# Causal side work moved between slots, buffers of the maxima and of the turned outputs exchanged, and a different plan for the first feed-forward

## The chip, the cores and the metric

The kernel runs on one core of a Trainium2 chip. The metric is device time in microseconds (us). A core has TensorE (PE, with its weight loads PEld), VectorE (DVE), ScalarE (ACT), GpSimd (POOL) and SyncE (SP), which here only issues DMAs. Each engine works through its own instructions in the order in which the program gives them.

## What is computed

Two blocks follow each other, each behind a layernorm and with a residual. All data are 32-bit floats. The first takes x of 4 × 1024 × 256:

```python
q, k, v = proj(wq, bq), proj(wk, bk), proj(wv, bv)      # 16 heads of 16
scores = einsum('bhqd,bhkd->bhqk', q, k) / sqrt(16)
attn = softmax(scores + causal_mask)
x = x + einsum('bhqk,bhkd->bhqd', attn, v) @ wo + bo    # on layernorm(x)
```

The second is a stack of two layers on the result's layernorm: attention of 8 heads of 64 in windows of 128 rows that look at their own and the previous window, with normalized and rotated q and k, and then a gated feed-forward (256 to 2 × 682, a × gelu(g), back to 256) behind a layernorm:

```python
h = shift_token(x); q, k, v = split(h @ wqkv)
x = x + local_attention(rotary_xpos(l2norm(q) * qs, l2norm(k) * ksc), v) @ wo
h = layernorm(shift_token(x)) * lg + lb; a, g = split(h @ w1 + b1)
x = x + (a * gelu(g)) @ w2 + b2
```

## The kernel before, in words

**Causal part.** The work is cut into chunks n = −1 to 15. Chunk n is batch b = n // 4 and head group c = n % 4 (4 heads of 16 rows, each in a strip of 32 partitions). Every chunk has 12 slots u. In a slot, `pair` (called twice, for two heads each) issues two kinds of score matmuls at L418: t, the transposed scores of chunk n, and s, the plain scores of chunk n + 1. Chunk −1, the prologue, has only s. From t, ScalarE makes exponentials (L442), and in the diagonal slots GpSimd zeroes what the mask forbids (affine_select, L448); `products` (L481) multiplies them with v two slots later. From s, VectorE takes row maxima, which are put into q as one more row of the contraction, so that the exponentials come out shifted. Slots 0 to 3 and 8 to 11 hold the diagonal piece: there the maximum is a tensor_tensor_reduce with the mask (L430), which also writes a full result that nobody reads, `junk`. In slots 4 to 7 it is a plain tensor_reduce (L436). The scores s and the helper matmuls share four PSUM banks (`pas`), so a matmul into a bank waits until VectorE has read what was there.

**Side work.** Everything else of the causal part is placed by hand: `put(n, u, function)` hangs a call behind slot u of chunk n, and a slot number of 12 or more runs into the next chunk. The functions are:

- `norm` (L258ff): mean and variance of tiles of the next batch on VectorE; `prep_x` (L275): the normalized tiles, on GpSimd for b > 0; `turn_x` (L298): 32 × 32 transposes on VectorE, and in its second call 16 DMAs that finish the transpose into xnT.
- `project`: projections of q and k, 16 matmuls at L252; `spread` (L377): DMAs of q and k rows into the strips; `prep_b`: v; `put_maxima` (L459): the maxima, by a transpose and DMAs.
- `put_out` (L494ff): the output turned by VectorE (L498), reciprocal of the sums (L500), multiplication on GpSimd (L501); `put_oT` (L506): turned back by VectorE into t3 (L510), and four DMAs into oT (L513).
- `out_b` (L517): the product with wo (pr, L252), then the residual: a copy by ScalarE (L533) and an addition by GpSimd (L534), or, for the last four tiles of the last batch, one addition by VectorE (L530). `out_s`: the statistics of the second layernorm (L541, L542); `out_c` (L557): its result into y_sb, on GpSimd.
- `clear_more` (L233 to L235): three memsets on GpSimd for the q and k buffers of later chunks.

The part runs in a manual schedule: each engine keeps the order in which the program calls. After the last slot, leftover side work, the last output and the last out_b, out_s, out_c follow (L694 to L705). Tile pools a1, a2, a4, a5 give 1, 2, 4, 5 buffers to a tag in turn.

**Window part.** One iteration n projects window n, and works on earlier windows: `stage` turns the rotated q and k of one window and the exponentials of another on VectorE (L864, L878), and then issues 16 DMAs into a ring (L895); `weigh` (plo, L1023) waits for them. The feed-forward of a group of four windows is cut into pieces, f_norm, f_hn, f_turn, six f_up (L1155) and four f_down (L1179, with the residual at L1184). `feed(n, place)`, called three times an iteration (place 0 to 2), issues the pieces whose number in F_PLAN is 3n + place − f_start(G); for the first group f_start is 17. If place 0 holds an f_down, it is fed ahead of stage, and otherwise behind it.

Of the kernel before, what the change touches and what calls it, by code (L numbers as in the profile page):

```python
# [10 lines left out]
F32 = mybir.dt.float32  # L11
# [39 lines left out]
def kernel_body(  # L51
# [122 lines left out]
    with actx:  # L174
# [159 lines left out]
        def bias():  # L334

            pb = one("pbias")
            for c in range(2):
                nc.tensor.transpose(
                    pb[:, c * P : (c + 1) * P], rows_c[:, 0, c * P : (c + 1) * P], ident
                )  # L340
            bv = a2.tile([P, 512], F32, tag="junk", name="bv")
            nc.scalar.copy(bv[:, 0:D], pb[:, 0:D])
            po = one("pbias_o")
            for c in range(2):
                nc.tensor.matmul(
                    po[:, 0:D], lhsT=bv[:, c * P : (c + 1) * P], rhs=wo_sb[:, c, :],
                    start=(c == 0), stop=(c == 1),
                )
            nc.vector.tensor_tensor(rows_c[:, 1, :], po[:, 0:D], rows_c[:, 1, :], ALU.add)
# [32 lines left out]
        def pair(n, u, pr):  # L382

            first, final = n < 0, n + 1 == NCH
            if (first or final) and pr:
                return
            th = () if first else range(4) if final else (2 * pr, 2 * pr + 1)  # L390
            sh = () if final else range(4) if first else (2 - 2 * pr, 3 - 2 * pr)

            def bank(pool, h):
                p, tag = ((pat, "t"), (pas, "s"))[pool]
                return p.tile([P, 512], F32, tag=tag, name=f"{'ts'[pool]}_{n}_{u}_{h}")

            todo = []
            if th:
                qb, kt = UNITS_T[u]
                c0 = max(0, kt * P - qb * 512)  # L400
                ts = {h: bank(final and h % 2, h) for h in th}
                for j, h in enumerate(th):
                    r = slice(32 * h, 32 * h + 32)
                    todo.append((j, 0, ts[h][:, c0:512], kTs(n)[r, kt * P : (kt + 1) * P],
                                 qTs(n)[r, qb * 512 + c0 : (qb + 1) * 512]))
            if sh:
                i, piece = UNITS_M[u]
                k0 = piece * 512
                k1 = min(k0 + 512, (i + 1) * P)
                w = k1 - k0  # L410
                diag = k1 == (i + 1) * P and piece == i // 4
                ss = {h: bank(not (first and h % 2), h) for h in sh}
                for j, h in enumerate(sh):
                    r = slice(32 * h, 32 * h + HD)
                    todo.append((j, 1, ss[h][:, 0:w], qTs(n + 1)[r, i * P : (i + 1) * P],
                                 kTs(n + 1)[r, k0:k1]))
            for j, _, o, lhsT, rhs in sorted(todo, key=lambda x: x[:2]):
                nc.tensor.matmul(o, lhsT=lhsT, rhs=rhs, start=True, stop=True)  # L418
            if sh:
                if i >= 4 and piece == 0 and pr == 0:  # L420
                    mxs[n + 1, i] = a5.tile([P, 4], F32, tag="mx", name=f"mx_{n + 1}_{i}")
                for h in sh:
                    first_of_two = i >= 4 and piece == 0
                    if first_of_two:
                        acc = mxs[n + 1, i][:, h : h + 1]
                    else:
                        acc = nmax[:, piece, 4 * h + i % 4 : 4 * h + i % 4 + 1]
                    if diag:
                        junk = a2.tile([P, 512], F32, tag="junk", name=f"junk_{n}_{u}_{h}")
                        nc.vector.tensor_tensor_reduce(  # L430
                            out=junk[:, 0:w], in0=ss[h][:, 0:w], in1=mask_c[:, 512 - w : 512],
                            scale=1.0, scalar=mxs[n + 1, i][:, h : h + 1] if piece else -3.0e38,
                            op0=ALU.add, op1=ALU.max, accum_out=acc,
                        )
                    else:
                        nc.vector.tensor_reduce(acc, ss[h][:, 0:w], AX.X, ALU.max)  # L436
                if piece and (pr or first):
                    del mxs[n + 1, i]
            for h in th:
                if h % 2 == 0:  # L440
                    et = a8.tile([P, 2, 512], F32, tag="et", name=f"et_{n}_{u}_{h}")
                nc.scalar.activation(et[:, h % 2, c0:512], ts[h][:, c0:512], AF.Exp, scale=ASCALE)  # L442
                if h % 2 == 0:
                    continue
                if kt >= 4 * qb:

                    d = et[:, :, c0 : c0 + P]
                    nc.gpsimd.affine_select(  # L448
                        out=d, in_=d, compare_op=ALU.is_ge, fill=0.0, base=0,
                        pattern=[[0, 2], [1, P]], channel_multiplier=-1,  # L450
                    )
                if h == 1:
                    avs_[n, u] = ([], c0)
                avs_[n, u][0].append(et)
# [51 lines left out]
        def put_oT(n, qb):  # L506

            b, c = divmod(n, NC4)
            t3 = a1.tile([P, 512], F32, tag="t3", name=f"t3_{n}_{qb}")
            nc.vector.transpose(t3, avs_.pop((n, "t1", qb)).rearrange("p q s -> p (q s)"))  # L510
            for j in range(4):
                r = (c % 2) * 64 + j * HD
                nc.sync.dma_start(  # L513
                    oT[r : r + HD, c // 2, qb * 512 : (qb + 1) * 512],
                    t3[STRIP * j : STRIP * j + HD, :],
                )

        def out_b(b, t2):
# [7 lines left out]
                        wo_sb[:, c, :], c,  # L526
                    )
            xt = xs[b][:, t0 : t0 + 2, :]
            if b == B - 1 and t2 >= 2:
                nc.vector.tensor_tensor(xt, pr.rearrange("p (i d) -> p i d", i=2), xt, ALU.add)  # L530
                return
            add = a1.tile([P, 2, D], F32, tag="add", name=f"add_{b}_{t2}")
# [33 lines left out]
        def put(n, u, fn, *a):  # L566

            plan[n + u // NU][u % NU].append((fn, a))

        def outs(n, u, b, t2):  # L570
            put(n, u, out_b, b, t2)
            put(n, u + 1, out_s, b, t2)
            put(n, u + 3, out_c, b, t2)

        def quarters(n, b, d, first, *slots):
            for i, u in enumerate(slots):
# [2 lines left out]
        for n in range(NCH):  # L579
            b, c = divmod(n, NC4)  # L580
            more = b + 1 < B
            if n >= 1:
                put(n, 2, put_out, n - 1, 1)
                put(n, 3, put_oT, n - 1, 1)
            if n + 1 < NCH:
                put(n, 4, put_maxima, n + 1, 0)
                put(n, 11, put_maxima, n + 1, 1)
            put(n, 6, put_out, n, 0)
            put(n, 7, put_oT, n, 0)
            if c == 0:  # L590
                if b:
                    quarters(n, b, 1, 3, 0, 2, 4, 6, 8)
                    outs(n, 7, b - 1, 2)
                    outs(n, NU, b - 1, 3)
                    put(n, 1, spread, n + 2, 0)
                    put(n, 3, spread, n + 3, 0)
# [4 lines left out]
                put(n, 9, spread, n + 2, 1)  # L601
                put(n, NU, spread, n + 3, 1)
            if c == 0 and more:
                for i, u in enumerate((5, 7, 9, 10)):
                    put(n, u, norm, b + 1, 2 * i, 2 * i + 2)
                put(n, 8, prep_x, b + 1, 0)
                put(n, 10, turn_x, b + 1, 0, 0)
                put(n, 10, prep_x, b + 1, 1)
                n += 1
                put(n, 0, turn_x, b + 1, 0, 1)  # L610
                put(n, 1, prep_x, b + 1, 2)
                put(n, 2, prep_x, b + 1, 3)
                put(n, 3, turn_x, b + 1, 1, 0)
                put(n, 4, turn_x, b + 1, 1, 1)
                quarters(n, b + 1, 0, 0, 5, 6, 8, 10)
                n += 1
                quarters(n, b + 1, 0, 4, 0, 2, 3, 4)
# [6 lines left out]
                quarters(n, b + 1, 1, 0, 3, 5, 7)  # L624
                n -= 3
            if c == 3:
                outs(n, 9, b, 0)
                outs(n, 11, b, 1)
        n = -1
        plan[n][0] = [(project, (0, 0, i, 3)) for i in range(2)]  # L630
        plan[n][0] += [(spread, (0, 1, nc.scalar)), (spread, (1, 0)), (spread, (1, 1))]
        put(n, 0, clear_more)
        put(n, 4, bias)
        put(n, 3, load_x, 1, 0, NW)
        put(n, 4, put_maxima, 0, 0)
# [15 lines left out]
        with tc.manual_schedule(  # L651
# [42 lines left out]
            for w in range(LAG, 0, -1):  # L694
                products(NCH - 1, NU - w)
            left = [x for u in plan[NCH] for x in u]
            for fn, a in left[0:1]:
                fn(*a)
            put_out(NCH - 1, 1)
            for fn, a in left[1:]:  # L700
                fn(*a)
            put_oT(NCH - 1, 1)
            for fn in (out_b, out_s, out_c):
                for t2 in (2, 3):
                    fn(B - 1, t2)  # L705
# [492 lines left out]
    }  # L1198
    F_END = max(F_PLAN)

    def f_start(G):

        sooner = 6 if G == 0 else 3 if G == len(groups) - 1 else 0
        return 3 * (GRP * G + GRP + 3) + 2 - sooner

    def feed(n, place, ask=False):

        if ask:
            return any(
                fn is f_down  # L1210
                for G in range(len(groups)) for fn, *_ in F_PLAN.get(3 * n + place - f_start(G), [])
            )
        for G in range(len(groups)):
            i = 3 * n + place - f_start(G)
            for fn, *a in F_PLAN.get(i, []):
                fn(G, *a)
            if G == len(groups) // DEPTH - 1:
                if i == 14:
# [139 lines left out]
```

## Time and profile before

| What | us |
|---|---|
| median of 3 runs | 1952.75 (1952.36 to 1958.35) |
| the profiled execution's own time | 1953.46 |
| its span, first to last instruction | 1951.7 |
| mean granted TensorE clock | 0.969 |
| PE / DVE / ACT / POOL busy | 1889.0 / 1347.7 / 1006.9 / 1029.7 |

The span starts at 0; the causal part runs to about 740 us, the window part from there. In the rows of the profile, the number with an x is a count of instructions. A timeline row gives the start, the duration, the engine, the line and what it writes and reads; in square brackets stands how long its engine had been idle before it, and what ended that. The clock of a stretch is the mean of the clock granted to TensorE: 1.00 is full speed, and where it is lower, some of the stretch ran at half speed.

### The profile page before, as it was taken

How to read it: one execution, taken by the hardware profiler on the slowest of the kernel's cores; microseconds unless marked ns; L12 is line 12 of the kernel's file. 1: busy time of each engine (PE TensorE's matmuls, PEld its weight loads, DVE VectorE, ACT ScalarE, POOL GpSimd, SP SyncE). 2: the span in 40 equal slices, each digit the busy share in tenths (PEclk: the TensorE clock that was granted, in tenths of full speed). 3: DMA queues.
4: the chain of work that ended last, by engine and by line, in shares of the span. 5: the costliest groups of instructions: out<-in, count | busy, mean ns of one | idle time of the engine just before them, and what ended most of it. 6: DMA issues, size and time to landing. Idle time of an engine off the chain costs nothing.

```text
span 1951.7 us, 51316 instructions
## 1 busy us (share of the span) xinstructions
PE 1889.0 (97%) x19258; PEld 1031.6 (53%) x19258; DVE 1347.7 (69%) x4092; ACT 1006.9 (52%) x2649; POOL 1029.7 (53%) x1268
## 2 busy tenths in 40 slices
PE   8999999999999978989899999999999999999899
PEld 4333333333333324656566666666666566566575
DVE  6866777677667835666776777776687687678633
ACT  1546555655656653554545555555545554555521
POOL 3222352245224247675765775675676676676621
PEclk8979999998999998999999999999999999999999
DMA  4022011202201011045555565556565555665520
GB/s 120 22 34 76 24 34 33 62 21 38 63 10 29 11 35 67 7 73 92 93 98 90 92 112 96 117 105 114 90 146 111 102 112 104 111 113 104 99 49 22
DMA packets 785127, 142.86 MB, mean 73 GB/s; under 512 B 753536, under 2 KB 775792, under 8 KB 784368
## 3 DMA queue, kind: packets, MB, share of 16 engines
q1 hardware_dynamic: 784624, 139.32, 36.8%
q8 instruction: 153, 2.51, 0.5%
q14 instruction: 94, 0.77, 0.1%
q10 hardware_dynamic: 256, 0.26, 0.1%
HBM read 21.25 MB, written 8.65 MB: 15 GB/s over the span
## 4 chain that ended last, share of the span: by engine, by line
PE 87%; DVE 4%; SPq 3%; POOL 2%; issue 2%; DMA 1%; ACT 1%; DVEq 0%; POOLq 0%; ACTq 0%
PE t L418 15%; PE pag L1155 15%; PE pf L1179 8%; PE av L481 7%; PE pw L1065 6%; PE pq L796 5%; PE pk L796 5%; PE pv L796 5%; PE plo L1023 4%; PE ls L943 4%; PE pp L252 3%; SPq L895 2%; PE pv L252 2%; PE s L418 2%; PE pr L252 2%
## 5 line engine op out<-in xcount | busy, mean ns | idle before, releaser
L442 ACT ACTIVATE et<-t 128x512 f32<-128x512 f32 (+2 forms) x744 | 327.8, 490 | 232.5 <-PE s L418 210.5
L418 PE MATMUL t<-qbuf,kbuf 32*128 32x512 f32 (+2 forms) x1488 | 396.7, 552 | 2.5 <-ACT et L442 2.4
L418 PE MATMUL s<-kbuf,qbuf 16*128 16x512 f32 (+3 forms) x1440 | 382.3, 554 | 1.3 <-DVE mx L436 0.9
L1155 PE MATMUL pag<-hnT,w 128*128 128x512 f32 x704 | 311.9, 592 | 0.8 <-DVE hnT L1139 0.8
L976 ACT ACTIVATE e<-e,lnmx 128x192 f32<-128x192 f32 (+2 forms) x512 | 224.1, 439 | 39.5 <-DVE lnmx L969 39.0
L418 PEld LDWEIGHTS t<-qbuf,kbuf 32*128 32x128 f32 x1488 | 144.1, 189 | 168.9 <-ACT et L442 111.5
L448 POOL TENSOR_SCALAR_AFFINE_SELECT et<-et 128x256 f32<-128x256 f32 x256 | 102.7, 408 | 225.0 <-ACT et L442 224.6
L990 POOL TENSOR_SCALAR e<-e,lrsum 128x192 f32<-128x192 f32 (+2 forms) x512 | 205.8, 425 | 19.9 <-DVE lrsum L987 14.3
L1155 PEld LDWEIGHTS pag<-hnT,w 128*128 128x128 f32 x704 | 131.5, 190 | 142.7 <-issue 135.1
L481 PE MATMUL av<-et,v_sb 128*32 128x256 f32 (+5 forms) x2240 | 186.9, 406 | 6.5 <-POOL et L448 4.7
L436 DVE TENSOR_REDUCE mx<-s 128x1 f32<-128x512 f32 x240 | 153.3, 682 | 56.5 <-PE s L418 54.3
L835 POOL TENSOR_TENSOR rn<-ss,mhalf 128x16 f32<-128x16 f32 x64 | 188.1, 2939 | 5.3
L1179 PE MATMUL pf<-w,act 128*128 128x256 f32 x768 | 173.1, 379 | 0.0
L832 POOL TENSOR_TENSOR rot<-rot,m 128x1024 f32<-128x1024 f32 x64 | 151.2, 2363 | 35.8 <-DVE m L813 30.1
L1179 PEld LDWEIGHTS pf<-w,act 128*128 128x128 f32 x768 | 145.8, 190 | 26.6 <-issue 7.2
L1169 DVE SCALAR_TENSOR_TENSOR act<-pag,cols_sb,ge 128x512 f32<-128x512 f32 x80 | 59.4, 743 | 141.8 <-ACT ge L1168 103.1
L430 DVE CUSTOM_DVE_ANT_0 junk<-s,mask_c 128x512 f32<-128x512 f32 (+3 forms) x240 | 106.8, 485 | 62.7 <-PE s L418 59.4
L418 PEld LDWEIGHTS s<-kbuf,qbuf 16*128 16x128 f32 x1440 | 142.0, 189 | 10.5 <-DVE mx L436 4.4
L430 DVE CUSTOM_DVE_ANT_0 junk<-s,mask_c,mx 128x512 f32<-128x512 f32 (+3 forms) x240 | 120.9, 546 | 37.6 <-PE s L418 36.4
L969 DVE CUSTOM_DVE_ANT_0 e<-ls,mask_h 128x192 f32<-128x192 f32 x408 | 116.8, 351 | 22.5 <-PE ls L943 22.5
L481 PEld LDWEIGHTS av<-et,v_sb 128*32 128x32 f32 x2240 | 45.4, 109 | 164.0 <-issue 113.4
L1065 PE MATMUL pw<-wlo,loT 128*128 128x256 f32 x512 | 127.7, 393 | 1.1 <-ACT loT L1056 0.7
(294 smaller groups left out, 3379.7 us busy)
## 6 DMA issues: line engine op xcount, KB each, us to landing
ring_sb<-turned SPq DMA_DIRECT2D x880, 96.0 KB
qbuf<-dense SPq DMA_DIRECT2D x128, 32.0 KB
oT<-t SPq DMA_DIRECT2D x128, 32.0 KB
x_keep<-x SPq DMA_DIRECT2D x4, 1024.0 KB
xr<-x_keep SPq DMA_DIRECT2D x8, 512.0 KB
out_dram<-y_sb SPq DMA_DIRECT2D x16, 256.0 KB
kbuf<-dense SPq DMA_DIRECT2D x120, 32.0 KB
x<-in_x_dram SPq DMA_DIRECT2D x3, 1024.0 KB
```

Of the source, the lines that this page charges most:

```text
L418: nc.tensor.matmul(o, lhsT=lhsT, rhs=rhs, start=True, stop=True)
L430: nc.vector.tensor_tensor_reduce(out=junk[:, 0:w], in0=ss[h][:, 0:w], in1=mask_c[:, 512 - w : 512], scale=1.0, scalar=mxs[n + 1, i][:, h : ...
L436: nc.vector.tensor_reduce(acc, ss[h][:, 0:w], AX.X, ALU.max)
L442: nc.scalar.activation(et[:, h % 2, c0:512], ts[h][:, c0:512], AF.Exp, scale=ASCALE)
L481: nc.tensor.matmul(av[32 * j : 32 * j + 32, lo:hi], lhsT=v_sb[b % 2][:, kt, VW * (4 * c + j) : VW * (4 * c + j) + STRIP], rhs=ets[j // 2][ ...
L796: nc.tensor.matmul(pq[i], lhsT=lhs[c], rhs=wt[:, c, i * INNER : (i + 1) * INNER], start=(c == 0), stop=(c == 1),)
L835: nc.gpsimd.tensor_tensor(rn[:, :, 0], ss, mhalf, ALU.pow)
L976: nc.scalar.activation(e[:, i, lo:nk], e[:, i, lo:nk], AF.Exp, bias=nmx[:, h : h + 1], scale=-1.0, accum_out=sums[:, h : h + 1],)
L990: nc.gpsimd.tensor_scalar(e[:, i, lo:nk], e[:, i, lo:nk], rsum[:, h : h + 1], 1.0, ALU.mult, ALU.mult)
L1065: nc.tensor.matmul(pw[:, 0:D], lhsT=oT[:, c, :], rhs=wt[:, c, :], start=(c == 0), stop=(c == 3))
L1155: nc.tensor.matmul(pg[half], lhsT=wt[:, c, ff * P : (ff + 1) * P], rhs=hnT[:, c, :], start=(c == 0), stop=(c == 1),)
L1179: nc.tensor.matmul(pf[:, 0:D], lhsT=act[:, f, i * P : (i + 1) * P], rhs=wt[:, f, :], start=(f == 0), stop=(f == NF - 1),)
```

## The change

1. `junk` has one buffer instead of two; t3, the output turned back, has two instead of one. The small tile bv takes the buffer of `add`.
2. Side work is placed in other slots: put_oT from slots 3 and 7 to 4 and 8; for c = 0, norm from 5, 7, 9, 10 to 3, 5, 7, 9, prep_x from 8, 10 and slots 1, 2 of the next chunk to 7, 9 and 0, 2 of it, turn_x from 10 and (next chunk) 0, 3, 4 to 10, 11 and (next chunk) 3, 5; out_s and out_c of out_b(b − 1, 2), which stays in slot 7, from 8 and 10 to 12 and 14; for c = 3, the first out_b from slot 9 to 10 with its out_s and out_c behind it, and out_s and out_c of the second, which stays in 11, from 12 and 14 to 13 and 15.
3. All residuals of the last batch are added by VectorE.
4. clear_more goes from slot 0 to slot 6 of the prologue chunk.
5. At the end of the causal part, put_out and put_oT of the last chunk come ahead of all leftover side work.
6. The first group of the feed-forward has a plan of its own, F_FIRST.

The program has as many instructions on TensorE and SyncE as before, two more on VectorE, two fewer on ScalarE and two fewer on GpSimd.

```diff
-            bv = a2.tile([P, 512], F32, tag="junk", name="bv")
+            bv = a1.tile([P, 512], F32, tag="add", name="bv")
...
-                        junk = a2.tile([P, 512], F32, tag="junk", name=f"junk_{n}_{u}_{h}")
+                        junk = a1.tile([P, 512], F32, tag="junk", name=f"junk_{n}_{u}_{h}")
...
-            t3 = a1.tile([P, 512], F32, tag="t3", name=f"t3_{n}_{qb}")
+            t3 = a2.tile([P, 512], F32, tag="t3", name=f"t3_{n}_{qb}")
...
-            if b == B - 1 and t2 >= 2:
+            if b == B - 1:
                 nc.vector.tensor_tensor(xt, pr.rearrange("p (i d) -> p i d", i=2), xt, ALU.add)
                 return
...
-        def outs(n, u, b, t2):
+        def outs(n, u, b, t2, wait=1):
             put(n, u, out_b, b, t2)
-            put(n, u + 1, out_s, b, t2)
-            put(n, u + 3, out_c, b, t2)
+            put(n, u + wait, out_s, b, t2)
+            put(n, u + wait + 2, out_c, b, t2)
...
-                put(n, 3, put_oT, n - 1, 1)
+                put(n, 4, put_oT, n - 1, 1)
...
-            put(n, 7, put_oT, n, 0)
+            put(n, 8, put_oT, n, 0)
...
-                    outs(n, 7, b - 1, 2)
+                    outs(n, 7, b - 1, 2, 5)
                     outs(n, NU, b - 1, 3)
...
             if c == 0 and more:
-                for i, u in enumerate((5, 7, 9, 10)):
+                for i, u in enumerate((3, 5, 7, 9)):
                     put(n, u, norm, b + 1, 2 * i, 2 * i + 2)
-                put(n, 8, prep_x, b + 1, 0)
+                put(n, 7, prep_x, b + 1, 0)
+                put(n, 9, prep_x, b + 1, 1)
                 put(n, 10, turn_x, b + 1, 0, 0)
-                put(n, 10, prep_x, b + 1, 1)
+                put(n, 11, turn_x, b + 1, 0, 1)
                 n += 1
-                put(n, 0, turn_x, b + 1, 0, 1)
-                put(n, 1, prep_x, b + 1, 2)
+                put(n, 0, prep_x, b + 1, 2)
                 put(n, 2, prep_x, b + 1, 3)
                 put(n, 3, turn_x, b + 1, 1, 0)
-                put(n, 4, turn_x, b + 1, 1, 1)
+                put(n, 5, turn_x, b + 1, 1, 1)
...
             if c == 3:
-                outs(n, 9, b, 0)
-                outs(n, 11, b, 1)
+                outs(n, 10, b, 0)
+                outs(n, 11, b, 1, 2)
...
-        put(n, 0, clear_more)
+        put(n, 6, clear_more)
...
             left = [x for u in plan[NCH] for x in u]
-            for fn, a in left[0:1]:
+            put_out(NCH - 1, 1)
+            put_oT(NCH - 1, 1)
+            for fn, a in left:
                 fn(*a)
-            put_out(NCH - 1, 1)
-            for fn, a in left[1:]:
-                fn(*a)
-            put_oT(NCH - 1, 1)
...
+    F_FIRST = {
+        1: [(f_norm,)], 3: [(f_hn,)], 6: [(f_turn,)], 7: [(f_up, 0)], 8: [(f_up, 1)],
+        9: [(f_up, 2)], 10: [(f_up, 3)], 12: [(f_up, 4)], 13: [(f_up, 5)], 16: [(f_down, 0)],
+        18: [(f_down, 1)], 20: [(f_down, 2)], 21: [(f_down, 3)],
+    }
+
+    def f_work(G, i):
+        return (F_PLAN if G else F_FIRST).get(i, [])
```

`feed` then asks f_work(G, i) where it asked F_PLAN.get(i, []). F_PLAN has f_up 0 to 5 at 7 to 12 and f_down 0 to 3 at 14 to 17.

More of the change, by code (lines that the diff above doesn't have):

```diff
@@ L1210, in feed @@
                 fn is f_down
-                for G in range(len(groups)) for fn, *_ in F_PLAN.get(3 * n + place - f_start(G), [])
+                for G in range(len(groups)) for fn, *_ in f_work(G, 3 * n + place - f_start(G))
             )
@@ L1214, in feed @@
             i = 3 * n + place - f_start(G)
-            for fn, *a in F_PLAN.get(i, []):
+            for fn, *a in f_work(G, i):
                 fn(G, *a)
```

## The prediction

> **What bounds the kernel now.** I read the page's busy line and its slices first: TensorE is busy for 97% of the span, so time can only come from its gaps or from stretches in which its clock is halved.
>
> ```profile
> PE 1889.0 (97%) x19258; PEld 1031.6 (53%) x19258; DVE 1347.7 (69%) x4092; ACT 1006.9 (52%) x2649; POOL 1029.7 (53%) x1268
> PEclk8979999998999998999999999999999999999999
> ```
>
> Then busy time by stretch (columns: PE, PEld, DVE, ACT, POOL busy us, granted clock, DMA share, GB/s):
>
> ```profile
> 85.00:130.00 45.00, 44.77 (x365) 16.37 (x360) 30.32 (x102) 20.44 (x48) 18.35 (x29) 0.70 0.23 41
> 135.00:175.00 40.00, 39.75 (x458) 14.85 (x456) 28.88 (x88) 25.25 (x58) 8.82 (x19) 1.00 0.14 31
> 265.00:310.00 45.00, 41.95 (x356) 15.30 (x358) 29.53 (x98) 19.96 (x46) 28.41 (x34) 0.81 0.21 36
> 445.00:490.00 45.00, 43.62 (x384) 16.06 (x384) 31.69 (x102) 22.23 (x49) 22.38 (x32) 0.85 0.21 35
> 715.00:742.00 27.00, 17.05 (x168) 8.02 (x161) 8.84 (x27) 4.22 (x13) 14.22 (x18) 0.81 0.12 45
> 900.00:1000.00 100.00, 91.72 (x1175) 60.76 (x1174) 71.18 (x222) 46.75 (x141) 60.68 (x70) 0.95 0.54 94
> 1000.00:1820.00 820.00, 818.30 (x8757) 522.75 (x8756) 606.60 (x1793) 434.82 (x1240) 555.35 (x602) 1.00 0.59 107
> ```
>
> From 1000 to 1820 us TensorE lacks 1.7 us: nothing to win there. The losses are chunks 1, 5 and 9 (c = 1; the first, third and fourth row), the handover near 729, and 900 to 1000. Chunk lengths, from first score matmul to first, are 49.8, 51.6 and 48.4 us for chunks 1, 5, 9. Chunk 14, without side work, is 35.4; a projection adds 0.65 to 0.85 and an out_b 1.6, so those three should take 38.8, 40.4 and 40.4. They lose 11.0, 11.2 and 8.0 us: 30 us bound what tidier side work can give.
>
> The timeline of chunk 1's start shows how that begins. The last rows of VectorE before it:
>
> ```profile
> 93.16 0.42 DVE L264 BATCH_NORM_STATS2 st<-x 128x6 f32<-128x256 f32 x1
> ...
> 94.44 0.76 DVE L298 STREAM_TRANSPOSE xturn<-xn 128x256 f32<-128x256 f32 x2
> 95.12 0.31 DVE L430 CUSTOM_DVE_ANT_0 junk<-s,mask_c,mx 128x128 f32<-128x128 f32 x1
> ```
>
> A norm (slot 10) and turn_x stand ahead of slot 11's maxima; their PSUM banks come free late, and chunk 1's first score matmuls, due at 94.26, start at 95.50. The clock halves at 97.3 and returns at 124.6, when slot 5's projection comes.
>
> **A rule against this change.** The Trainium skill (TensorE: Matmul & The Clock Gate, "HAM oscillation — how this bites in real kernels") says that the clock falls when TensorE idles over about 3.4 us. Here it idles 0.23 of 45 us and still runs at 0.70. By the rule these stretches are not caused by late VectorE work and the change gains 0 of the 30 us; by the rows, narrow matmuls that are staggered are little enough work to halve it. The row decides: side work is worth up to 11 us in chunk 1.
>
> **1. Side work (norm, prep_x, turn_x, out_s, put_oT).** From the rows: a norm of two tiles is 1.45 us of VectorE, turn_x 0.69, put_oT 0.66, out_s 1.28. After the change slots 8 to 11 of chunk 0 hold put_oT, norm, turn_x, turn_x instead of nothing, norm, norm + turn_x, and slot 0 of chunk 1 loses a turn_x. VectorE's sequence, from the trace's times for the scores: norm to 84.1, slot 8's four maxima (0.67 each) to 86.8, put_oT 87.5, slot 9's (scores ready 89.12) 90.2, norm 91.55, slot 10's (0.40 each) 93.2, turn_x 93.9, two of slot 11's (0.27) 94.5. So far its first banks come free at 94.5 instead of 95.5: no stall.
>
> **2. One junk buffer for the masked maxima (L430).** New: each L430 must wait for the one before it, because it writes the same buffer; 436 of 512 wait so in the changed program. Before, with two buffers, one waits for the last but one, which has long ended, and neighbours overlap:
>
> ```profile
> 84.64 0.74 DVE L430 CUSTOM_DVE_ANT_0 junk<-s,mask_c,mx 128x512 f32<-128x512 f32 x1
> 85.31 0.08 DVE L430 DVE_READ_ACCUMULATOR2_ANT nmax<- 128x1 f32 x1
> 85.31 0.75 DVE L430 CUSTOM_DVE_ANT_0 junk<-s,mask_c,mx 128x512 f32<-128x512 f32 x1
> ```
>
> The pitch is 0.67. The nearest dependent pair is the statistics of out_s:
>
> ```profile
> 722.55 0.37 DVE L541 BATCH_NORM_STATS2 sto<-x 128x6 f32<-128x256 f32 x1
> 722.95 0.18 DVE L542 BATCH_NORM_AGGREGATE mvo<-sto 128x2 f32<-128x6 f32 x1
> 723.05 0.39 DVE L541 BATCH_NORM_STATS2 sto<-x 128x6 f32<-128x256 f32 x1
> ```
>
> The dependent one starts 0.03 after its predecessor's end (722.92), the independent one 0.08 before. A dependent L430 would so start at 85.39 + 0.03 = 85.42: 0.11 each. Bounds: 0 from below (a wait can't speed it), 0.19 from above (another dependent pair, at 738.24, was 0.11 apart: 0.08 + 0.11). The skill (VectorE: DVE Perf Modes, "The DRAIN you can't avoid") measured that semaphores between chained operations cost nothing: by it this part is 0. I take 0.11, since the rows show the overlap that the wait ends.
>
> In the prologue chunk VectorE has no cover: it is busy 6.87 of 7.20 us from 21.0 and 7.78 of 8.10 from 47.1, where its 32 masked maxima are. 32 × 0.11 = **+3.5 us** (0 to +6.1). A later chunk's 32 have TensorE as cover: VectorE has 28.88 of 40 us, 32.4 with them. The exception is slots 8 to 11 of c = 0. Step 1's sequence with 0.11 more for each maximum: slot 8's to 87.2, put_oT 87.9, slot 9's 90.45, norm 91.8, slot 10's 93.8, turn_x 94.5, two of slot 11's 95.27. That is against 95.50 now. Behind the waiting L430 in VectorE's queue are norms, put_out and maxima; score matmuls wait for its banks.
>
> So the delay of chunk 1's first scores shortens from 1.24 to about 1.0 us. Is that enough? Relating matmul work (rows × columns × N) to the clock, every 3.4 us stretch at or below 17.4 (in percent of the array) was followed by half clock, none at 19.6 or above; this stretch has 16.4 to 17.1, and attention runs at 21 to 26. A quarter of a us less waiting adds 0.25 / 3.4 × 25 = 1.8: 18.2 to 18.9, between the two. I call it slightly more likely than not that the clock holds; then chunk 1 gets back **−8.5** of its 11.0 (bounds −11 and +2).
>
> **3. Chunks 5 and 9** have another cause too: GpSimd's backlog. In chunk 5, put_oT's transpose stands in front of the reductions for 5.57 us, waiting for L501:
>
> ```profile
> 293.52 0.71 DVE L510 STREAM_TRANSPOSE t<-t 128x512 f32<-128x512 f32 x1 [5.57 <-DMA xnT<-xturn]
> ```
>
> (It names a DMA; L501 on GpSimd ended at 293.50.) In slots 0 to 3 GpSimd now gets one more out_c (2.44 us, moved from slot 10) and less prep_x; my sum for it is 16.3 us against 12.5 of TensorE. put_oT a slot later gives back 2.5 of those 3.8. **−1 us** for both together (−12 to +8).
>
> **4. Handover.** The chain of waits shows pr waiting for oT:
>
> ```profile
> PE pr L252 <- DMA oT<-t: 8.5, 1, 8.5
> PE plo L1023 <- DMA ring_sb<-turned: 7.4, 5, 2.6
> ```
>
> Before it GpSimd does out_c (722.14 to 724.54), then L501 to 725.16, then the transpose 725.19, then the DMAs; oT lands at 729.84. With put_out and put_oT first, L501 starts when the reciprocal is done (722.63) instead of 724.54: **−1.9 us**. out_c then comes 0.6 us later; pr's 6.04 us cover it. The residuals of t2 = 0, 1 on VectorE: 2 × 0.69, beside TensorE: 0, and take 1.27 us each from GpSimd.
>
> **5. First feed-forward.** Windows 8 to 14 are a chain of stage, 16 ring DMAs (11.5 us of issue) and weigh, about 16.7 us a round. Stage 11 was late:
>
> ```profile
> 903.87 0.42 DVE L1184 TENSOR_TENSOR y_sb<-pf,y_sb 128x256 f32<-128x256 f32 x1 [2.33 <-PE pf L1179]
> 904.27 1.25 DVE L864 STREAM_TRANSPOSE turned<-rot 128x1024 f32<-128x1024 f32 x1
> ```
>
> Of window 10, which stands ahead of it, two f_downs go (5.34 us of TensorE) and one f_up comes (1.72): 5.34 − 1.72 = 3.6 us sooner. The downs then fall into windows 11 and 12, whose gaps before plo are 3.3 us in all. TensorE-bound from 1000 on, so kept: **−3.6** (0 to −5).
>
> **6. The rest.** Clearing (3 memsets of 0.95): from 13.36, where prep_x runs beside it, 3.75 us for four, to idle GpSimd behind 35. But pxn's copy at 17.42 waits for ScalarE's DMA issue to 17.38: 0 (−0.4 to +0.3). Two t3 buffers, bv in another buffer: no wait of that kind in the trace, 0. xnT's 16 DMAs now stand in front of spreads in SyncE's queue, some 10 us; the spreads' readers are a chunk away: 0; were that cover gone, up to 3.
>
> **Sum.** +3.5 − 8.5 − 1 − 1.9 − 3.6 = −11.5. The profiled execution took 1953.46 us (span 1951.7), 0.7 over the median of 1952.75. 1953.46 − 11.5 = 1942.0; against the median 1941.3. I say 1941.5.
>
> **Rivals.**
> - *The stall stays* (chance 0.24): chunk 1 gives 0, the rest stands: +3.5 + 0 − 1 − 1.9 − 3.6 = −3.0, so 1950. For it: 95.27 is close to 95.50. Against: the margin is on the good side.
> - *The wait costs nothing*, as the skill has it (0.12): prologue 0, chunk 1 −10, chunks 5 and 9 −5: −20.5, so 1933. Against: the overlap in the rows.
> - *Slower* (0.22): one mechanism, L430's wait. At 0.19 the prologue pays 6.1; some 14 such waits precede slot 11's banks, so they come free at 95.27 + 14 × 0.08 = 96.4, later than now. Half clock then starts earlier and lasts longer in chunks 1, 5 and 9, some +4 each, and out_s in slot 0 (1.28) adds to it: 6.1 + 12 − 5.5 = +12.6, so 1965. It decides from about 0.11 + 0.23 / 14 = 0.127 us a wait. For it: the margin is small, and GpSimd's backlog helps it. Against: one row only has 0.11 between dependents.
>
> **Numbers.** Forecast 1936 to 1946: 0.42. What a measurement can tell from no change is 0.3%, 5.9 us: 1946.9 to 1958.6. Faster: 0.42 + 0.12 + 0.04 of the second case's edge = 0.58; slower 0.22; same 0.20. The range 1930 to 1963 leaves out the slow rival's upper half and the fast one's lower edge, some 0.15; on the fast side alone it would be 1930 to 1947.
>
> **What would show it.** Right: clock 0.95 or more from 85 to 130 us; L430's pitch at 128x512 at 0.78 and the prologue chunk 3.5 us longer than 34.8; pr's wait for oT 6.5 us; stage 11 some 3.5 us sooner relative to window 8. Wrong: a clock of 0.7 again in chunk 1 (then 1950), a pitch of 0.86 (then slower), a pitch of 0.67 (then 1933), or half clock in chunks that had none.

## The result, and the profile after

Four runs of the changed kernel gave 1961.75 to 1989.57 us, median 1981.55, against 1952.55 before: ratio 1.0138, interval 1.0102 to 1.0173. Slower, where I had forecast 1941.5. A later set of 22 runs of the same program gave 1944.41 to 1990.16, median 1956.46, against 1951.97 before on that chip: ratio 1.0023, interval 1.0002 to 1.0043. The ratios leave out executions more than 1.5% above the fastest of their kernel, four of those 22, so the second one reads lower than a ratio of all would. Both say slower. That they differ so much fits the changed kernel's time, which spreads over 46 us from execution to execution, where 35 runs of the kernel before spread over 18; whether the chip adds to it is not known. What has to be explained is a loss and a spread.

The busy line and the clock line of the profiled execution (1989.57 us, span 1987.8):

```profile
PE 1925.6 (97%) x19258; PEld 1044.4 (53%) x19258; DVE 1372.9 (69%) x4094; ACT 1004.4 (51%) x2647; POOL 1029.6 (52%) x1266
...
PEclk8969988999999579989999999999999999999999
```

TensorE has as many matmuls as before and is busy 36.6 us longer, as much as the span grew (36.1); the clock line has a hole of 5 and 7 tenths at slices 14 and 15 that was not there. Busy time by stretch says where, in the columns used before; the last row is chunk 14 and the end of 13:

```profile
88.00:133.00 45.00, 44.75 (x348) 16.75 (x343) 30.68 (x99) 19.44 (x46) 17.88 (x28) 0.67 0.16 31
...
455.00:500.00 45.00, 43.77 (x460) 17.50 (x456) 37.56 (x118) 25.18 (x58) 23.42 (x34) 1.00 0.23 41
620.00:680.00 60.00, 59.75 (x468) 21.20 (x464) 38.09 (x115) 26.48 (x60) 16.67 (x29) 0.69 0.08 17
680.00:735.00 55.00, 54.90 (x420) 19.90 (x416) 32.53 (x100) 23.44 (x56) 8.96 (x21) 0.66 0.08 26
```

Chunk 1 ran at half clock as before, chunk 9 (second row) no longer did, and chunks 13 and 14, which were at full speed before, ran at half from 642 to 717 us. The masked maxima in the timeline of the prologue chunk, before and after:

```profile
21.09 0.69 DVE L430 CUSTOM_DVE_ANT_0 junk_-1_0_0_349<-s_-1_0_0_341,mask_c 128x512 f32<-128x512 f32 x1 [3.88 <-PE t_-1_0_3_344 L418]
21.70 0.08 DVE L430 DVE_READ_ACCUMULATOR2_ANT nmax<- 128x1 f32 x1
21.70 0.69 DVE L430 CUSTOM_DVE_ANT_0 junk_-1_0_1_351<-t_-1_0_1_342,mask_c 128x512 f32<-128x512 f32 x1
```

```profile
22.09 0.69 DVE L430 CUSTOM_DVE_ANT_0 junk_-1_0_0_349<-s_-1_0_0_341,mask_c 128x512 f32<-128x512 f32 x1 [7.21 <-PE t_-1_0_3_344 L418]
22.71 0.08 DVE L430 DVE_READ_ACCUMULATOR2_ANT nmax<- 128x1 f32 x1
22.94 0.69 DVE L430 CUSTOM_DVE_ANT_0 junk_-1_0_1_351<-t_-1_0_1_342,mask_c 128x512 f32<-128x512 f32 x1
```

The next one starts 0.85 us after the first; before, the same pair had a pitch of 0.61 (21.09 and 21.70). After the accumulator's read ends (22.79) VectorE stands still for 0.15. The wait costs 0.23 to 0.24 us, twice what I took and more than my upper bound. It is so throughout: of 384 pairs of neighbouring masked maxima of one width, 286 overlapped before and none after, where 349 have a gap of 0.1 to 0.2 us behind the read.

The chain of waits where the tail was changed, to be set beside 8.5 and 7.4:

```profile
PE pr L252 <- DMA oT<-t: 7.3, 2, 6.7
PE plo L1021 <- DMA ring_sb<-turned: 5.6, 5, 1.4
```

Chunk lengths, from first score matmul to first, of the profiled executions (chunks not listed agree within 1 us):

| kernel | −1 | 0 | 1 | 4 | 5 | 8 | 9 | 12 | 13 | 14 | its time |
|---|---|---|---|---|---|---|---|---|---|---|---|
| before | 34.8 | 39.6 | 49.8 | 40.9 | 51.6 | 40.6 | 48.4 | 39.6 | 37.0 | 35.4 | 1953.46 |
| changed | 41.1 | 40.8 | 50.2 | 42.1 | 52.5 | 41.9 | 41.7 | 40.6 | 55.5 | 49.5 | 1989.57 |
| changed, again | 40.4 | 41.7 | 39.2 | 41.9 | 48.5 | 41.9 | 43.5 | 40.6 | 38.7 | 36.9 | 1946.66 |
| before, one junk buffer | 36.9 | 41.0 | 51.0 | 43.5 | 51.6 | 43.2 | 46.6 | 41.0 | 38.8 | 36.4 | 1965.0 |
| changed, two junk buffers | 32.1 | 39.2 | 39.2 | 39.7 | 47.3 | 39.7 | 40.6 | 39.4 | 37.0 | 35.4 | 1921.57 |
| and tables in chunk 14 | 32.1 | 39.1 | 39.5 | 39.7 | 41.4 | 39.7 | 45.3 | 39.3 | 37.0 | 35.4 | 1924.0 |
| changed, maxima in place | 38.1 | 39.2 | 39.9 | 39.9 | 48.4 | 39.9 | 41.0 | 39.4 | 37.0 | 35.4 | 1929.9 |

### The profile page after: what moved, and what is told of

It reads as the page before. It is cut to its first block, busy times and chain, and to the rows that moved or that the text cites. A ratio compares the mean times of both kernels' runs of the same rounds, so it can differ in the third digit from the quotient of the medians.

```text
span 1987.8 us, 51388 instructions
## 1 busy us (share of the span) xinstructions
PE 1925.6 (97%) x19258; PEld 1044.4 (53%) x19258; DVE 1372.9 (69%) x4094; ACT 1004.4 (51%) x2647; POOL 1029.6 (52%) x1266
## 3 DMA queue, kind: packets, MB, share of 16 engines
q1 hardware_dynamic: 784624, 139.32, 36.1%
## 4 chain that ended last, share of the span: by engine, by line
PE 90%; DVE 3%; SPq 2%; POOL 2%; issue 1%; ACT 1%; DMA 1%; DVEq 0%; ACTq 0%; POOLq 0%
PE t L418 17%; PE pag L1153 14%; PE av L481 8%; PE pf L1177 8%; PE pw L1063 6%; PE pq L794 5%; PE pk L794 5%; PE pv L794 5%; PE plo L1021 4%; PE ls L941 3%; PE pp L252 3%; SPq L893 2%; PE s L418 2%; PE pv L252 2%; PE pr L252 2%
## 5 line engine op out<-in xcount | busy, mean ns | idle before, releaser
L418 PE MATMUL t<-qbuf,kbuf 32*128 32x512 f32 (+2 forms) x1488 | 412.8, 587 | 1.4 <-ACT et L442 1.2
L418 PE MATMUL s<-kbuf,qbuf 16*128 16x512 f32 (+3 forms) x1440 | 411.2, 589 | 2.4 <-DVE nmax L430 1.8
L974 ACT ACTIVATE e<-e,lnmx 128x192 f32<-128x192 f32 (+2 forms) x512 | 224.2, 439 | 41.3 <-DVE lnmx L967 40.8
L418 PEld LDWEIGHTS t<-qbuf,kbuf 32*128 32x128 f32 x1488 | 149.4, 200 | 175.9 <-ACT et L442 113.8
L481 PE MATMUL av<-et,v_sb 128*32 128x256 f32 (+5 forms) x2240 | 197.0, 426 | 4.4 <-POOL et L448 3.1
L430 DVE CUSTOM_DVE_ANT_0 junk<-s,mask_c,mx 128x512 f32<-128x512 f32 (+3 forms) x240 | 131.7, 549 | 55.9 <-PE s L418 29.5
L418 PEld LDWEIGHTS s<-kbuf,qbuf 16*128 16x128 f32 x1440 | 153.3, 201 | 9.2 <-DVE nmax L430 4.5
L430 DVE CUSTOM_DVE_ANT_0 junk<-s,mask_c 128x512 f32<-128x512 f32 (+3 forms) x240 | 116.8, 487 | 55.0 <-PE s L418 30.2
L481 PEld LDWEIGHTS av<-et,v_sb 128*32 128x32 f32 x2240 | 46.6, 113 | 179.6 <-issue 138.1
```

The costliest lines, as they stand in the source:

```text
L430: nc.vector.tensor_tensor_reduce(out=junk[:, 0:w], in0=ss[h][:, 0:w], in1=mask_c[:, 512 - w : 512], scale=1.0, scalar=mxs[n + 1, i][:, h : ...
L481: nc.tensor.matmul(av[32 * j : 32 * j + 32, lo:hi], lhsT=v_sb[b % 2][:, kt, VW * (4 * c + j) : VW * (4 * c + j) + STRIP], rhs=ets[j // 2][ ...
L974: nc.scalar.activation(e[:, i, lo:nk], e[:, i, lo:nk], AF.Exp, bias=nmx[:, h : h + 1], scale=-1.0, accum_out=sums[:, h : h + 1],)
```

## The experiments

**One junk buffer in the kernel before.** The reverse of the next experiment:

```diff
-                        junk = a2.tile([P, 512], F32, tag="junk", name=f"junk_{n}_{u}_{h}")
+                        junk = a1.tile([P, 512], F32, tag="junk", name=f"junk_{n}_{u}_{h}")
```

> The kernel before with one thing changed: one buffer for the unread result of the masked maxima (bv in the buffer of add, as in the changed kernel). Theory W (the wait of each masked maximum for the one before it is the cost, about 0.23 us each as the changed kernel's pitch shows): pitch 0.84 at 128x512, prologue chunk 41 instead of 34.8 us, chunks 0, 4, 8, 12 about 1 us longer each, 1962 to 1968 us; above 1985 if chunk 13 loses its clock as in the changed kernel. Theory S (the moved side work is the cost, the wait only pays in the prologue): 1959 us, all chunks from 0 on as before.

Measured: ratio 1.0093 (1.0072 to 1.0114), median 1971.13. The wait alone makes the kernel slower, by some 18 us. Every chunk with c = 0 is 1.4 to 2.6 us longer, and 13 and 14, which have little else for VectorE, 1.8 and 1.0. The prologue chunk took 36.9, not 41. Above the expected 1962 to 1968, on theory W's side.

**Two junk buffers in the changed kernel**, and one for t3 again, since both do not fit:

```diff
-                        junk = a1.tile([P, 512], F32, tag="junk", name=f"junk_{n}_{u}_{h}")
+                        junk = a2.tile([P, 512], F32, tag="junk", name=f"junk_{n}_{u}_{h}")
-            t3 = a2.tile([P, 512], F32, tag="t3", name=f"t3_{n}_{qb}")
+            t3 = a1.tile([P, 512], F32, tag="t3", name=f"t3_{n}_{qb}")
```

> The changed kernel with two buffers for the masked maxima and one for t3 again; all moved side work, the tail and the feed-forward plan stay. Theory W: prologue chunk 34.8 us, chunks 13 and 14 back to 37.0 and 35.4, the tail's -1.9 and -3.6 kept, chunks 1, 5, 9 together 0 to 25 us shorter than before: 1925 to 1949 us. Theory S: chunks 13 and 14 still run at half clock (out_s in slot 0 is there), about 1975 us.

Measured: ratio 0.9870 (0.9850 to 0.9891), median 1928.07, six runs within 8.3 us. Chunks 1 and 9, and then chunks 13 and 14, by stretch:

```profile
92.00:131.00 39.00, 37.89 (x408) 14.86 (x401) 31.00 (x98) 23.41 (x54) 14.01 (x26) 1.00 0.24 40
...
428.00:469.00 41.00, 39.28 (x444) 14.78 (x438) 33.88 (x111) 24.67 (x57) 21.69 (x33) 1.00 0.23 39
594.00:666.00 72.00, 70.89 (x760) 27.66 (x760) 58.81 (x184) 43.96 (x100) 22.55 (x43) 1.00 0.09 22
```

All are at full clock: the moved side work does what part 1 of the prediction said, once VectorE does not wait. Theory S, that the moved side work is the cost by itself, is out.

**The maxima written in place.** To take the wait away without touching t3, the masked maximum writes its unread result over the scores in PSUM:

```diff
-                            out=junk[:, 0:w], in0=ss[h][:, 0:w], in1=mask_c[:, 512 - w : 512],
+                            out=ss[h][:, 0:w], in0=ss[h][:, 0:w], in1=mask_c[:, 512 - w : 512],
```

> The changed kernel without a junk buffer: the masked maxima write their full result over the scores in PSUM, so none waits for the one before it; t3 keeps two buffers. If the wait of one junk buffer is all that was wrong with the change: as with two junk buffers, 1922 to 1932 us, pitch 0.6 to 0.67 at 128x512. If writing PSUM costs time as the wait did: pitch 0.75 or more, 1950 us or above.

Measured: ratio 0.9885 (0.9866 to 0.9905), median 1928.38; the timeline of the prologue chunk:

```profile
23.72 0.73 DVE L429 CUSTOM_DVE_ANT_0 t_-1_0_1_342<-t_-1_0_1_342,mask_c 128x512 f32<-128x512 f32 x1
24.37 0.14 DVE L429 DVE_READ_ACCUMULATOR2_ANT nmax<- 128x1 f32 x1
24.37 0.73 DVE L429 CUSTOM_DVE_ANT_0 s_-1_0_2_343<-s_-1_0_2_343,mask_c 128x512 f32<-128x512 f32 x1
```

The overlap is back (pitch 0.65), with t3 in two buffers. So two ways of removing the wait give the same time within the intervals. They differ in t3's buffers and in what a maximum takes (0.65 against 0.61), so a small effect of the second t3 buffer is not ruled out.

**The tail alone**: in the kernel before, only the order after the last slot and F_FIRST, in the diff's own words.

> The kernel before with the last output ahead of the leftover side work and the plan of its own for the first feed-forward group, nothing else. Both theories: 1.9 us less from chunk 15's first score to pr, 3.6 less from pr to window 14, 1947 us; if either is lost again later, 1949 to 1953.

Measured: ratio 0.9978 (0.9964 to 0.9991), median 1949.02 of 22. A real gain, 3.3 us in the medians where 5.5 was expected. In its profile pr waits 6.64 us for oT instead of 8.47, and window 14 starts 5.0 us sooner after pr; from there to the end it takes 2.7 us longer than the kernel before. So the expectation's second case holds, some of the gain is lost again later.

**The statistics back** (one junk buffer):

```diff
-                    outs(n, 7, b - 1, 2, 5)
+                    outs(n, 7, b - 1, 2)
```

> The changed kernel (one junk buffer) with out_s and out_c of out_b(b - 1, 2) back in slots 8 and 10 instead of 12 and 14. If chunk 13 loses its clock because this out_s (1.28 us of VectorE) meets the wait of the masked maxima in slots 0 to 2: chunks 13 and 14 take some 38.8 and 36.4 us as in the run with one junk buffer alone, 1955 to 1962 us. If the wait alone does it: still 50 or more each, 1985 us. Chunks 5 and 9 in both cases 48 to 53.

Measured: median 1962.54, ratio 1.0065 (1.0042 to 1.0088), 13 runs from 1950.12 to 1986.24. In its profile chunk 13 took 38.8 and chunk 14 36.9, as the first theory has it, but chunk 9 took 44.7 where 48 or more was expected, and chunk 1, which the edit doesn't touch, 39.1. After the next experiment these lengths say nothing on the out_s: they are one draw. What the trace does say of it comes at the end of that experiment.

**The changed kernel once more**, unchanged.

> The changed kernel as it is, once more: its four runs lay between 1961.75 and 1989.57 us. If that spread is chunks 13 and 14, whose clock falls in some executions only (the stretch before had 17.8% of the array's work, where the records have falls at 17.4 and none at 19.6): times in two groups, near 1960 and near 1988, and this profile shows chunk 13 either at 39 or at 55 us, the other chunks as before within 2 us. If not: chunk 13 at 55 in this profile too whatever its time.

Measured: the 22 runs of the result's second set; no two groups, but a broad spread. The profile is of an execution of 1946.66 us: chunk 1 took 39.2 instead of 50.2, chunk 13 38.7 instead of 55.5, chunk 14 36.9 instead of 49.5. One program, no edit, and chunk 13 is not alone in it. VectorE's rows around the start of chunk 1 (102.8 and 103.1 us), first in the 1989.57 us execution, then in this one:

```profile
101.75 0.77 DVE L298 STREAM_TRANSPOSE xturn<-xn 128x256 f32<-128x256 f32 x2
102.44 0.31 DVE L430 CUSTOM_DVE_ANT_0 junk<-s,mask_c,mx 128x128 f32<-128x128 f32 x1
...
105.09 0.66 DVE L430 CUSTOM_DVE_ANT_0 junk<-s,mask_c 128x512 f32<-128x512 f32 x1
```

```profile
102.06 0.77 DVE L298 STREAM_TRANSPOSE xturn<-xn 128x256 f32<-128x256 f32 x2
102.75 0.31 DVE L430 CUSTOM_DVE_ANT_0 junk<-s,mask_c,mx 128x128 f32<-128x128 f32 x1
...
105.40 0.65 DVE L430 CUSTOM_DVE_ANT_0 junk<-s,mask_c 128x512 f32<-128x512 f32 x1
```

They are 0.31 us apart from start to end: VectorE is equally late in both. The stretch of 30 us that follows:

```profile
100.00:130.00 30.00, 29.75 (x204) 11.82 (x206) 18.23 (x63) 11.33 (x28) 12.77 (x20) 0.55 0.21 38
```

```profile
100.00:130.00 30.00, 29.55 (x296) 12.45 (x295) 25.28 (x78) 17.07 (x39) 13.65 (x21) 1.00 0.22 41
```

In all twelve traces every stretch between two changes of the clock lasts a whole multiple of 3.413 us (the last one, cut off by the end, apart), so each trace shows where its windows of 3.413 us begin. I count a window's work as rows × columns × moving elements over its matmul records, two to a matmul. 100% of a window stands for 128 × 128 × 8192; full-size matmuls back to back at full clock, a record every 0.43 us in the next experiment, would hold 50.

In the longer execution (first row) the clock fell at 102.9, and the window from 99.5 had held 14.9%. In the other, windows began at 97.4 and 100.8, about 1 us later against VectorE's work, and held 22.3 and 20.7. A window cut there as in the longer one, from 99.8, would have held 15.1. The same delay, cut differently, falls below the limit or not.

Chunk 13 is open to this in some kernels only. Where chunks 13 and 14 kept full clock, the sparsest 3.413 us in them, whatever the phase, held 20.7 or 20.8% in the seven traces without the wait, and 17.8 or 17.9% in the four with it, each time from about 9.9 us into chunk 13. The window after which it fell in the 1989.57 us execution began 9.9 us into it as well. In the twelve traces the clock fell after every window under 15.8% and after none of 18.4% or more. So the kernel decides that chunk 13 can fall, and the phase whether it does. The starts that give less than 18.4% span 0.36 to 0.38 of the 3.413 us. An estimate from that, with all phases equally likely, is one execution in nine; 3 of the 22 took more than 1980 us. The four traces include the kernel before with one junk buffer and the one with the statistics back, so the place of out_s does not change this.

**Matmuls for the clock's sake.** Three full-size matmuls that nobody reads, first in slots 4 and 8 of chunk 13 and slot 4 of chunk 14 of the changed kernel:

```diff
+        def heat(n, u):
+            ph = one(f"heat_{n}_{u}")
+            for _ in range(3):
+                nc.tensor.matmul(ph, lhsT=ident, rhs=mask_c, start=True, stop=True)
```

> The changed kernel with three matmuls of 128x128 by 512 added, whose result nobody reads, in slots 4 and 8 of chunk 13 and slot 4 of chunk 14. If chunks 13 and 14 are long because the clock stays at half for want of dense work: it returns within a slot or two of the first or second of them, chunks 13 and 14 take 40 to 45 and 37 us instead of 55.5 and 49.5, 1962 to 1968 us. If they are long because TensorE waits for VectorE: no gain, up to 8 us more than 1989.

Measured: median 1969.35 of five (1961.44 to 1976.76), ratio 1.0080 (1.0047 to 1.0113). In its profile chunks 13 and 14 took 42.8 and 39.1 us with the clock at 1.00 throughout, so it shows no recovery: with this spread it does not tell whether the clock would have fallen.

```profile
630.00:674.00 44.00, 43.75 (x404) 17.48 (x404) 33.17 (x103) 22.89 (x53) 15.41 (x27) 1.00 0.09 19
674.00:713.00 39.00, 38.44 (x370) 15.47 (x366) 29.87 (x89) 21.80 (x50) 7.63 (x18) 1.00 0.08 26
```

Then in the kernel before, behind slot 1 of chunks 1, 5 and 9:

> The kernel before with three matmuls of 128x128 by 512, whose result nobody reads, behind slot 1 of chunks 1, 5 and 9; the norms and turn_x stay where they were. If the clock is what those chunks lose (so that their late scores only cost by halving it): chunk 1 some 42 to 44 us instead of 49.8, chunks 5 and 9 2 to 4 us shorter, 1938 to 1946 us. If the waits for VectorE and GpSimd are: 4 us more than before for the added matmuls, 1956 us.

Measured: ratio 1.0003 (0.9985 to 1.0020): no change in the time. In its profile chunk 1's clock was halved for 10.2 us instead of 27.3 and the chunk took 46.1 instead of 49.8. The burst brings the clock back, as the first theory has it, but 3.7, 2.9 and 2.0 us in three chunks of one execution did not show in the median. In that execution the part from chunk 15 to the end took 1264.4 us, where three others with the same tail took 1255.9 to 1258.4; the clock was halved at other places. Whether that is chance or follows from the bursts stays open.

**The tables late**: from the kernel with two junk buffers, GpSimd's two scalings of the rotary tables (2.37 us each) out of chunk 5:

```diff
-        put(5, 0, scale_tab, 0, 0)
-        put(5, 1, scale_tab, 0, 1)
+        put(14, 1, scale_tab, 0, 0)
+        put(14, 3, scale_tab, 0, 1)
```

> The changed kernel with two junk buffers and one for t3, and the two scalings of the rotary tables (2.37 us of GpSimd each) in slots 1 and 3 of chunk 14 instead of 0 and 1 of chunk 5. If GpSimd's backlog makes chunk 5 long: 41 us there instead of 47.3, 1922 us. If VectorE's does: chunk 5 still 47, 1928 us.

Measured: median 1923.82, ratio 0.9864 (0.9845 to 0.9883), the lowest median of this study. Chunk 5 with two junk buffers alone, then chunk 5 and chunk 9 of this kernel:

```profile
256.00:304.00 48.00, 45.72 (x448) 16.47 (x448) 34.28 (x113) 24.63 (x57) 26.47 (x36) 0.86 0.22 39
...
256.00:298.00 42.00, 40.27 (x444) 15.29 (x447) 34.32 (x113) 24.81 (x57) 21.73 (x33) 1.00 0.23 40
422.00:468.00 46.00, 44.27 (x446) 15.94 (x448) 34.15 (x113) 24.72 (x57) 21.78 (x33) 0.89 0.23 40
```

Chunk 5 is at full clock and takes 41.4 us; without this edit it took 47 or more in each of the eleven executions profiled. GpSimd's backlog was its cause, as far as one execution can show. Chunk 9 fell in this execution (45.3) and not in the one of the kernel it is derived from (40.6), so the gain in chunk 5 is not clear in the times: the medians are 4 us apart and the intervals of the ratios overlap.

**Clearing alone**: put(n, 6, clear_more) for put(n, 0, clear_more) in the kernel before.

> The kernel before with clear_more in slot 6 of the prologue instead of slot 0, nothing else. As predicted: 0, 1952 us, four prep_x in 1.4 us instead of 3.75, the first scores no earlier since ScalarE's copies wait for its DMA issue. Rival: the prologue chunk is 2.7 us shorter as in the run with two junk buffers, where it took 32.1, 1949.5 us.

Measured: ratio 1.0023 (1.0009 to 1.0036). The four prep_x take 1.39 us instead of 3.75, and pxn's copies still wait for ScalarE's DMA issue:

```profile
13.47 1.39 DVE L275 TENSOR_SCALAR xn<-x,mv,rs_a 128x256 f32<-128x256 f32 x4 [1.13 <-POOL rs_a L161]
...
15.48 2.60 ACTq L377 DMA_DIRECT2D kbuf<-dense  x4
18.12 1.07 ACT L288 COPY xnT<-pxn 128x512 f32<-128x512 f32 x2 [2.71 <-DMA kbuf<-dense]
```

So no gain, as predicted, for the reason predicted. But it came out 0.23% slower, and that stays open. In its profile ScalarE's issue began 0.70 us later than before (15.48 against 14.78); the clock's first rise, at 6.69 us against 5.13, was already late, ahead of the memsets. Chunks −1, 5 and 9 were 1.3, 2.0 and 2.5 us longer.

## Why the prediction was wrong

**The step that failed is part 2**: "I take 0.11, since the rows show the overlap that the wait ends", with 0.19 as the bound. The nearest dependent pair was BATCH_NORM_STATS2 and its AGGREGATE, 0.03 us from end to start. Between two masked maxima stands the read of the accumulator, and a maximum that has to wait for that read starts 0.15 after its end: 0.23 in all. The pair was near in form, and wrong in its price. The rule that I weighed against the rows (the Trainium skill, VectorE: DVE Perf Modes, "The DRAIN you can't avoid": semaphores between chained operations cost nothing, measured there with tensor_copy) is further off still for this instruction: the chip shows 0.23 a wait, and 18 us for the kernel.

Carried through my own sequence of slots 8 to 11, 0.23 frees slot 11's banks at 95.27 + 14 × 0.12 = 97.0, 1.5 us later than before and far past the point from which the slow rival decides (0.11 + 0.23 / 14 is 0.126; I had written 0.127). **The slow rival had the right mechanism**, L430's wait and the half clock that follows; I had given it 0.22. Where it strikes was not as it said, and neither was my sequence: in the changed kernel's trace chunk 1's first plain scores start 0.05 us after its first transposed ones, where it was 1.24, and chunk 0 is 1.2 us longer instead.

The rival expected chunks 1, 5 and 9 to get longer by 4 us each; they were 0.9 us longer at most, and some shorter, since the moved side work helps there at the same time. In the longer execution the loss came in chunks 13 and 14 (+18.5 and +14.1 of the 36.1), where no projection or out_b brings the clock back: there I had costed the waits as covered by TensorE, with 32.4 of 40 us. That sum holds on average even at 0.23 (36.2 of 40), and did not hold for the 3.413 us from 638.8 (17.8% of the array's work) that decided. **That cover is the second thing that failed**: TensorE was busy all through those 3.413 us, and lost its clock. Half clock in chunks that had none was among the signs of being wrong that I had named.

**Point by point.** Prologue chunk: predicted +3.5; measured +6.3 and +5.6 in two executions of the changed kernel, +2.1 with one junk buffer alone. Its clock is halved for different times in each, and without any edit there the run with matmuls in chunks 1, 5 and 9 took 32.4 us where the kernel before took 34.8; so the size of this term is not measured. Side work in chunk 1: −8.5 predicted, +0.4 in one execution, −10.6 in the other; −10.6 without the wait. Chunks 5 and 9: −1 predicted for both; +0.9 and −6.7, or −3.1 and −4.9. Handover: −1.9 predicted; from chunk 15's first score to pr it went from 36.5 to 34.6 us, −1.9. Feed-forward: −3.6 predicted; from pr to the first projection of window 14 it went from 214.6 to 211.1, −3.55. The handover was right: the four traces with the old order have 36.5, the eight with the new one 34.6 or 34.7. That the feed-forward came out to a tenth is luck: the same stretch takes 212.4 to 216.4 us in four traces with the old plan and 208.4 to 212.9 in eight with the new, and from window 14 to the end the changed kernel took 1.0 us longer, so not all was kept; the tail alone gave 3.3 us in the medians. The clearing gave no gain, as I had said, but alone it was 0.23% slower, which I had not. Attention holds more of the array's work than the 21 to 26 of my part 2: 21 to 33 in chunks 13 and 14 of the kernel before, out_b's window apart.

**What I missed altogether** is that the clock's fall belongs to an execution; the kernel only opens a stretch to it. I forecast one time where the change makes a spread: the profile of one execution could show that a stretch held 16.4 to 17.1% and fell, but not how near the neighbouring stretches, with all phases of the window, were to it. The rule that I set against the change (the Trainium skill, TensorE: Matmul & The Clock Gate, "HAM oscillation — how this bites in real kernels": an idle stretch of some 3.4 us) is not what is at work here: in the 60 us from 620 TensorE idles 0.25 us and runs at 0.69.

## What to carry to other kernels

Before a scratch buffer goes from two to one, ask what its writer then waits for: an output that nobody reads still serializes its writers, and here that took 0.23 us from each of hundreds of instructions that had overlapped. Price such a wait from the same instruction, not from a neighbour. Where narrow matmuls run close to the clock's limit, a delay's price is decided by its phase: look at stretches without dense work first, for there a fallen clock stays down, and judge by many executions, since one profile shows one draw.

## What the runs showed of the hardware

- Over the twelve traces the clock halved after every 3.413 us window at full clock with less than 15.8% of the array's work (111 windows; rows × columns × moving elements, counted as above), after none with 18.4% or more, and between these in 37 of 43. Whether the chip counts just this is not shown. It came back only after windows with 18.0% or more: in chunks 13 and 14, at half clock, 21 windows in a row held 12.9 to 18.0 and it stayed down for 75 us. At full clock the same two chunks hold 21 or more in the kernel before, so they are stable up there, and stable down there too.
- A masked maximum that writes its full result to PSUM over its input took 0.73 us against 0.69 with the result in SBUF, and its accumulator read 0.14 against 0.08; the pitch went from 0.61 to 0.65 us.
